# Layout of the stationary operand, the plan's lags and the end of a graph-network kernel on one Trainium2 core

## The chip, the cores and the metric

The kernel runs on one NeuronCore of a Trainium2 chip. The metric is the device time of one execution in microseconds. A ratio in this text is the mean time of one kernel's fast runs over the mean time of the other kernel's fast runs of the same rounds, with a 95% interval; it is therefore not quite the ratio of the medians that are quoted beside it. All runs here are of the fast state; small differences remain in the mean granted TensorE clock (0.989 to 0.998), and one section below is about them.

## The reference

Four layers on `x` of shape (64, 256, 128), all float32. The first three are graph convolutions with one 256 x 256 adjacency `adj`; each ends in `layernorm(x + layer(x))`. The fourth is a gated graph network of five steps, and most of the work is there:

```python
def step(h, _):
    m_in = jnp.einsum('nm,bmd->bnd', in_matrix, h)      # in_matrix = out_matrix = adj
    m_out = jnp.einsum('nm,bmd->bnd', out_matrix, h)
    av = jnp.concatenate([m_in, m_out], axis=-1)
    u3 = h @ u3_w.T + u3_b
    z = jax.nn.sigmoid(av @ w3_w.T + w3_b + u3)
    r = jax.nn.sigmoid(av @ w4_w.T + w4_b + u3)
    hv = jnp.tanh(av @ w5_w.T + w5_b + (r * h @ u5_w.T + u5_b))
    h = (1.0 - z) * h + z * hv
    return (h, None)
# ...
x = _layernorm(x + _L3_gnn_ref(x, adj, adj, ..., 5), axis=-1)
```

## The kernel before

The 64 batch entries form 32 groups of two. The kernel first writes down every operation of every group with a cost, a lag and its dependences (class `Plan`). A greedy simulation on the host, at build time, then orders them, and the instructions are emitted in that order. So **the plan's costs and lags are not executed; they only set the order on each engine**. On the chip an engine waits where the next operand of its list is late: in the trace of this kernel SyncE waited 138.6 us, in 85 waits, with a load of `h` for the write `dh` to land, and in the six traces compared below all its planned DMAs come in the planned order.

```python
ACTIVE = 6      # groups in flight
HEAD = 2        # the first groups turn x by TensorE
TAIL = 4        # the last groups turn h by TensorE (the "PE path")
...
    def add(self, engine, cost, lag, rank, run, reads=(), writes=(), after=()):
        op = Op(len(self.ops), rank, engine, cost, lag, run, [*reads, *writes])
...
def dve_cost(elements):
    return elements / 0.96 + 75          # 608 ns for 512 elements
```

The 608 ns are a number of the plan; in the trace VectorE's operations on 512 elements a partition took 683 to 723 ns by mean, and the transpose `th` of `hT`, which writes with a stride, 1111.

A step needs h in both orientations: `hT` (features on partitions) for the gates, and `h` (nodes on partitions) as the stationary operand of the propagation. `hT` is what the step produces. In most groups the way back to `h` is: VectorE transposes block by block (`th`, 1111 ns by mean), a DMA writes the blocks to DRAM (`dh`, 2.0 us from issue to landing by median), and a DMA reads them back in another order (`h`, 2.8 us). In the last `TAIL` groups TensorE transposes `hT` into PSUM instead (`pth`, four matmuls 109 ns apart) and ScalarE copies it out (586 ns by mean).

```python
        def turned(self, name, src, ins, outs):
            t, far = self.val("w", "t" + name), self.val("dram", "d" + name)
            self.dve(dve_cost(512), lambda: nc.vector.transpose(t.ap.rearrange(outs, k=4, q=Q),
                                                                src.ap.rearrange(ins, k=4, q=Q)), [src], [t])
            self.add("SP", 420, 2000, lambda: nc.sync.dma_start(far.ap, t.ap), [t], [far])
            return far

        def packed(self, name, src):
            far = self.turned(name, src, "p (k q i) -> p q k i", "p (k j q) -> p q k j")
            t = self.val("w", name)

            def run():
                nc.sync.dma_start(t.ap.rearrange("p (r n) -> p r n", r=4),
                                  far.ap.rearrange("(r i) (k n) -> (i k) r n", r=4, k=4))

            self.add("SP", 420, 2350, run, [far], [t])
            return t
...
    def by_node(v):                       # every 4th element of a row: 16 bytes apart
        return v.ap.rearrange("p (n q) -> p q n", q=Q)
...
            for s in range(STEPS):
                m = self.propagate(f"g{s}", h, ats, ins, outs)      # pmg, stationary operand h
                # ... pr, ph: ten matmul records of 512 columns; r, rh, z, hv; d, e ...
                hT = self.tensor(f"hT{s}", OP.add, hT, e)
                if g < G - TAIL:
                    if s < STEPS - 1:
                        h, ats, ins = self.packed(f"h{s}", hT), a1p, by_node
                else:
                    pT = self.transposes(f"h{s}", hT)
                    if s < STEPS - 1:
                        h = self.copied(f"h{s}", pT)
```

The four values of q in a row of `h` are interleaved there, so that the reading DMA can move runs of 512 bytes. The price is the stride in `by_node`: a weight load of this `h` takes 326 ns by mean, one of `y`, which lies in natural order, 190. (`a1p` is the adjacency with its rows in the order in which this DMA delivers the nodes; the views call it `aTp`.)

Of the kernel before, what the change touches and what calls it, by code (L numbers as in the profile page):

```python
# [14 lines left out]
NB = 2  # L15
ACTIVE = 6
HEAD = 2
TAIL = 4
STEPS = 5
EPS = 1e-5  # L20
BANKS = 8
# [20 lines left out]
class Plan:  # L42
# [7 lines left out]
        self.ops, self.slots = [], slots  # L50

    def add(self, engine, cost, lag, rank, run, reads=(), writes=(), after=()):
        op = Op(len(self.ops), rank, engine, cost, lag, run, [*reads, *writes])
        op.deps.update(after)
        for v in reads:
            op.deps.add(v.writer)
            v.readers.append(op)
        for v in writes:
            if v.writer is not None:
                op.deps.add(v.writer)  # L60
            op.deps.update(v.readers)
            v.writer, v.readers = op, []
        op.deps.discard(op)
        for v in op.vals:
            if op not in v.users:
                v.users.append(op)
        self.ops.append(op)
        return op
# [69 lines left out]
def act_cost(elements):  # L138
    return elements / 1.2 + 165
# [3 lines left out]
def kernel(  # L143
# [30 lines left out]
    nc = tc.nc  # L174
# [3 lines left out]
    Q = NB * T  # L178
# [125 lines left out]
    def nat(v):  # L304
        return v.ap.rearrange("p (q c) -> p q c", q=Q)
# [17 lines left out]
    class Group:  # L323
# [12 lines left out]
            return op  # L336

        def pe(self, cost, run, reads, writes):
            return self.add("PE", cost, 200, run, reads, writes)

        def dve(self, cost, run, reads, writes):
            return self.add("DVE", cost, 130, run, reads, writes)

        def act(self, run, reads, writes, cost=act_cost(512)):
            return self.add("ACT", cost, 70, run, reads, writes)

        def copied(self, name, ps, kind="w"):
            t = self.val(kind, name)
# [82 lines left out]
        def packed(self, name, src):  # L431


            far = self.turned(name, src, "p (k q i) -> p q k i", "p (k j q) -> p q k j")
            t = self.val("w", name)

            def run():
                nc.sync.dma_start(t.ap.rearrange("p (r n) -> p r n", r=4),
                                  far.ap.rearrange("(r i) (k n) -> (i k) r n", r=4, k=4))

            self.add("SP", 420, 2350, run, [far], [t])
            return t

        def product(self, ps, w, rhs, start, stop, shared=False):
# [13 lines left out]
        def record(self):  # L458
# [14 lines left out]
            for t in range(T):  # L473
                p = self.val("bank", f"py0{t}")
# [48 lines left out]
            h = y  # L523
            outs = None
            if g < G - TAIL:
                hT = self.brought("hT", self.turned("h", h, "p (q k j) -> p q k j", "p (k q i) -> p q k i"))
                outs = by_block
            else:
                pT = self.transposes("h", h)
                hT = self.val("w", "hT")  # L530
                self.dve(dve_cost(512), lambda t=hT, p=pT: nc.vector.tensor_copy(t.ap, p.ap), [pT], [hT])
            ats, ins = a1, None
            for s in range(STEPS):
                m = self.propagate(f"g{s}", h, ats, ins, outs)
                pr = self.val("bank", f"pr{s}")
                self.product(pr, u3T, hT, True, False)
                self.product(pr, w4T, m, False, True)
                r = self.gate_(f"r{s}", pr, AF.Sigmoid, rb)
                rh = self.tensor(f"rh{s}", OP.mult, r, hT)
                ph = self.val("bank", f"ph{s}")  # L540
                self.product(ph, w5T, m, True, False)
                self.product(pr, w34T, m, False, True, shared=True)
                z = self.gate_(f"z{s}", pr, AF.Sigmoid, zb)
                self.product(ph, u5T, rh, False, True)
                hv = self.gate_(f"hv{s}", ph, AF.Tanh, hb)

                d = self.tensor(f"d{s}", OP.subtract, hv, hT)
                e = self.tensor(f"e{s}", OP.mult, z, d)
                hT = self.tensor(f"hT{s}", OP.add, hT, e)
                if g < G - TAIL:  # L550
                    if s < STEPS - 1:
                        h, ats, ins = self.packed(f"h{s}", hT), a1p, by_node
                else:
                    pT = self.transposes(f"h{s}", hT)
                    if s < STEPS - 1:
                        h = self.copied(f"h{s}", pT)
            if g < G - TAIL:
                pT = self.brought("hn", self.turned("n", hT, "p (k q i) -> p q k i", "p (k q j) -> p q k j"))
                add = self.residual("3", pT, y, lambda v: v.ap.rearrange("p (r q j) -> p q r j", r=4, q=Q),
                                    lambda v: v.ap.rearrange("p (q r j) -> p q r j", r=4, q=Q))  # L560
            else:
                add = self.residual("3", pT, y)
            o = self.normalise("3", *add)
            self.add("SP", 450, 2700, lambda: nc.sync.dma_start(view(out, g), nat(o)), [o], [])

    a1 = [aT[:, kt, :] for kt in range(T)]
    a2 = [a2T[:, kt, :] for kt in range(T)]
    a1p = [aTp[:, kt, :] for kt in range(T)]
# [53 lines left out]
```

## Time and profile before

| | before |
|---|---|
| time, median of its first runs | 1457.4 us (1457.2 to 1458.1) |
| profiled span | 1455.1 us |
| TensorE busy | 97% |
| VectorE / ScalarE / GpSimd busy | 69% / 35% / 16% |
| DMA queue of SyncE, share of 16 engines | 26.2% |

The page's first part gives busy time, share of the span and number of instructions of each engine; its second part cuts the span into 40 slices and gives the busy tenths of each. In the views PE is TensorE, PEld its weight loads, DVE VectorE, ACT ScalarE, POOL GpSimd and SP SyncE. A line of the groups view reads: source line, engine, operation, out<-in by the program's names, shapes, count; then busy time in us and the mean duration of one in ns; then the idle time of the engine just before these instructions and what ended it. All matmuls come from one helper line, so the tile names tell them apart: `pmg` is the propagation in the gated network, `pr` and `ph` its gates, `pth` a transpose.

One measure in this text is not a line of a view: **PE's stalls**. Matmul durations overlap (those of `pmg<-aTp,h` are 402 ns by mean and start 233 ns apart), so I take the times from each matmul's start to the next one's, and take the median for each kind (mostly 216, 233, 429 or 109 ns); this median is called the pitch. The sum of the medians is the length that PE's stream would have without a wait; everything above it is stall. For the kernel before the sum is 5.4 us to the first matmul, 1391.2 us of medians, 50.1 us of stalls, and 8.4 us after the start of the last matmul: 1455.1 us.

### The profile page before, as it was taken

The numbers are of one execution on the slowest core, as the hardware profiler recorded it, in microseconds if no ns is written. First come the engines' busy times: TensorE is split into PE (matmuls) and PEld (weight loads), VectorE is DVE, ScalarE is ACT, GpSimd is POOL, SyncE is SP. The second block draws the span as 40 slices with busy tenths as digits, with TensorE's granted clock in tenths as the row PEclk, the third lists the DMA queues.
The fourth block names the chain that finished last, engine by engine and source line by source line (L and its number), as shares of the span: only waits on it lengthen the run. The fifth ranks groups of instructions, "written<-read, shape, count | busy, mean of one in ns | idle before, by whom it ended". The sixth has DMA issues, their size and how long they took to land.

```text
span 1455.1 us, 16313 instructions
## 1 busy us (share of the span) xinstructions
PE 1407.4 (97%) x5054; PEld 965.1 (66%) x5054; DVE 1008.5 (69%) x2696; ACT 515.7 (35%) x820; POOL 230.7 (16%) x199
## 2 busy tenths in 40 slices
PE   5999999999999999999999999999999999999995
PEld 4866676567666777667676667676677676656652
DVE  3756686758777686676876677776767768757734
ACT  1143423333333333333333333334333333344342
POOL 0411031101210122001211022111111112001200
PEclk9999999999999999999999999999999999999998
DMA  5022232323233223233222333223333322210000
GB/s 165 15 81 79 92 111 87 113 68 109 77 111 109 94 96 107 73 123 95 95 82 90 104 105 96 82 94 95 111 103 96 97 79 88 74 42 30 1 8 15
DMA packets 173830, 123.44 MB, mean 85 GB/s; under 512 B 12592, under 2 KB 148144, under 8 KB 173744
## 3 DMA queue, kind: packets, MB, share of 16 engines
q1 hardware_dynamic: 171440, 121.16, 26.2%
q10 hardware_dynamic: 2304, 1.25, 0.3%
q8 instruction: 40, 0.66, 0.2%
q14 instruction: 46, 0.38, 0.1%
HBM read 61.80 MB, written 60.29 MB: 84 GB/s over the span
## 4 chain that ended last, share of the span: by engine, by line
PE 47%; DVE 5%; DMA 1%; ACT 1%; issue 0%; POOL 0%; SPq 0%; POOLq 0%; DVEq 0%; ACTq 0%
PE pr L191 15%; PE pmg L191 10%; PE ph L191 10%; PE py L191 7%; PE pm L191 3%; PE pmq L191 1%; DVE y L382 1%; DMA h<-dh 1%; DVE d L455 1%; DVE e L455 1%; PE pth L406 1%; DVE st L357 1%; DVE hT L455 1%; ACT hv L449 0%; DVE s L373 0%
## 5 line engine op out<-in xcount | busy, mean ns | idle before, releaser
L368 POOL TENSOR_TENSOR rs<-ve,half 128x4 f32<-128x4 f32 x128 | 141.3, 1106 | 1120.3 <-DVE ve L362 1112.5
L191 PEld LDWEIGHTS pmg<-aTp,h 128*128 128x128 f32 x896 | 220.5, 326 | 39.0 <-DMA h<-dh 12.6
L191 PE MATMUL pmg<-aTp,h 128*128 128x256 f32 x896 | 231.1, 402 | 6.0 <-DMA h<-dh 5.6
L455 DVE TENSOR_TENSOR d<-hv,hT 128x512 f32<-128x512 f32 x160 | 114.3, 715 | 170.6 <-ACT hv L449 170.4
L455 DVE TENSOR_TENSOR rh<-r,hT 128x512 f32<-128x512 f32 x160 | 112.3, 702 | 143.2 <-ACT r L449 143.0
L349 ACT COPY mg<-pmg 128x512 f32<-128x512 f32 x160 | 93.7, 585 | 280.0 <-PE pmg L191 264.8
L382 DVE TENSOR_SCALAR y<-s,mv,rs 128x128 f32<-128x128 f32 x512 | 146.0, 350 | 56.5 <-POOL rs L368 56.0
L191 PE MATMUL pr<-hT,u3T 128*128 128x512 f32 x320 | 163.5, 596 | 3.5 <-DVE hT L455 3.1
L191 PE MATMUL pr<-mg,w4T 128*128 128x512 f32 x320 | 164.4, 595 | 2.3 <-ACT mg L349 2.3
L191 PE MATMUL pr<-mg,w34T 128*128 128x512 f32 x320 | 163.0, 594 | 0.1
L191 PE MATMUL ph<-mg,w5T 128*128 128x512 f32 x320 | 162.8, 592 | 0.0
L191 PE MATMUL ph<-rh,u5T 128*128 128x512 f32 x320 | 162.5, 593 | 0.0
L449 ACT ACTIVATE r<-pr,rb 128x512 f32<-128x512 f32 x160 | 110.0, 687 | 137.5 <-PE pr L191 129.0
L449 ACT ACTIVATE z<-pr,zb 128x512 f32<-128x512 f32 x160 | 109.9, 687 | 133.3 <-PE pr L191 128.4
L449 ACT ACTIVATE hv<-ph,hb 128x512 f32<-128x512 f32 x160 | 109.9, 687 | 48.3 <-PE ph L191 46.4
L414 DVE STREAM_TRANSPOSE th<-hT 128x512 f32<-128x512 f32 x112 | 124.4, 1111 | 1.4
L455 DVE TENSOR_TENSOR e<-z,d 128x512 f32<-128x512 f32 x160 | 115.6, 723 | 3.8
L455 DVE TENSOR_TENSOR hT<-hT,e 128x512 f32<-128x512 f32 x160 | 109.6, 686 | 2.5
L357 DVE BATCH_NORM_STATS2 st<-s 128x6 f32<-128x128 f32 x512 | 109.4, 278 | 1.2
L191 PEld LDWEIGHTS ph<-rh,u5T 128*128 128x128 f32 x320 | 60.4, 190 | 72.6 <-issue 56.9
L191 PEld LDWEIGHTS ph<-mg,w5T 128*128 128x128 f32 x320 | 60.8, 190 | 70.3 <-issue 56.7
L191 PEld LDWEIGHTS pr<-mg,w4T 128*128 128x128 f32 x320 | 59.0, 191 | 51.2 <-issue 43.8
(95 smaller groups left out, 1609.5 us busy)
## 6 DMA issues: line engine op xcount, KB each, us to landing
dh<-th SPq DMA_DIRECT2D x140, 256.0 KB, 2.0
h<-dh SPq DMA_DIRECT2D x112, 256.0 KB, 2.8
x<-in_x_dram SPq DMA_DIRECT2D x32, 256.0 KB, 3.4
out_dram<-y SPq DMA_DIRECT2D x32, 256.0 KB, 2.3
dx<-tx SPq DMA_DIRECT2D x30, 256.0 KB, 2.1
xT<-dx SPq DMA_DIRECT2D x120, 64.0 KB, 2.0
hT<-dh SPq DMA_DIRECT2D x112, 64.0 KB, 2.0
dn<-tn SPq DMA_DIRECT2D x28, 256.0 KB, 2.0
```

The costliest lines, as they stand in the source:

```text
L191: nc.tensor.matmul(o, lhsT, rhs, start=start, stop=stop, skip_group_check=shared)
L349: self.act(lambda: nc.scalar.copy(t.ap, ps.ap), [ps], [t])
L357: nc.vector.bn_stats(st.ap[:, q * 6:(q + 1) * 6], nat(s)[:, q, :])
L368: lambda: nc.gpsimd.tensor_tensor(rs.ap, ve.ap, half, op=OP.pow), [ve], [rs])
L382: nc.vector.tensor_scalar(nat(y)[:, q, :], nat(s)[:, q, :], mv.ap[:, 2 * q:2 * q + 1], rs.ap[:, q:q + 1], op0=OP.subtract, op1=OP.mult)
L406: nc.tensor.transpose(ps.ap[:, q * P:(q + 1) * P], src.ap[:, q * P:(q + 1) * P], ident)
L414: self.dve(dve_cost(512), lambda: nc.vector.transpose(t.ap.rearrange(outs, k=4, q=Q), src.ap.rearrange(ins, k=4, q=Q)), [src], [t])
L449: self.act(lambda: nc.scalar.activation(t.ap, ps.ap, func, bias=bias, scale=1.0), [ps], [t], act_cost(512) + 100)
L455: self.dve(dve_cost(512), lambda: nc.vector.tensor_tensor(t.ap, a.ap, b.ap, op=op), [a, b], [t])
```

## The change

The intent is to have `h` lie in natural order, so that the weight load reads a contiguous row; to tell the plan that results and transfers arrive later than it believed; and to use the PE path for the last two groups only.

```diff
-TAIL = 4
+TAIL = 2
...
     def add(self, engine, cost, lag, rank, run, reads=(), writes=(), after=()):
+        if engine == "SP":
+            lag += 700
...
-            return self.add("PE", cost, 200, run, reads, writes)
+            return self.add("PE", cost, 260, run, reads, writes)
...
-            return self.add("DVE", cost, 130, run, reads, writes)
+            return self.add("DVE", cost, 260, run, reads, writes)
...
-            return self.add("ACT", cost, 70, run, reads, writes)
+            return self.add("ACT", cost, 130, run, reads, writes)
...
-            far = self.turned(name, src, "p (k q i) -> p q k i", "p (k j q) -> p q k j")
+            far = self.turned(name, src, "p (k q i) -> p q k i", "p (k q j) -> p q k j")
...
-                nc.sync.dma_start(t.ap.rearrange("p (r n) -> p r n", r=4),
-                                  far.ap.rearrange("(r i) (k n) -> (i k) r n", r=4, k=4))
-
-            self.add("SP", 420, 2350, run, [far], [t])
+                f = far.ap.rearrange("(r i) (k q j) -> q (i k) r j", r=4, k=4, q=Q)
+                for q in range(Q):
+                    nc.sync.dma_start(nat(t)[:, q, :].rearrange("p (r j) -> p r j", r=4), f[q])
+
+            self.add("SP", 2570, 2000, run, [far], [t])
...
-                        h, ats, ins = self.packed(f"h{s}", hT), a1p, by_node
+                        h, ats, ins = self.packed(f"h{s}", hT), a1p, nat
```

The last SP line matters later: with the new load the plan also gets new figures for it, 1.8 us more than for the old one.

## The prediction

> **What bounds the kernel now.** I read the page's busy shares first, then the busy slices.
>
> ```profile
> span 1455.1 us, 16313 instructions
> PE 1407.4 (97%) x5054; PEld 965.1 (66%) x5054; DVE 1008.5 (69%) x2696; ACT 515.7 (35%) x820; POOL 230.7 (16%) x199
> PE   5999999999999999999999999999999999999995
> ...
> q1 hardware_dynamic: 171440, 121.16, 26.2%
> ```
>
> TensorE is busy in every slice but the first and last; VectorE has 31% to spare and the DMA queue of SyncE fills 26% of the DMA engines. So only three things can shorten the run: cheaper PE work, fewer PE stalls between 50 and 1350 us, and a shorter start or end. But ends of matmuls are modelled, so "busy" hides a slow stream. I therefore went to the groups by shape.
>
> ```profile
> L191 PE MATMUL pmg<-aTp,h 128*128 128x256 f32 x896 | 231.1, 402 | 6.0 <-DMA h<-dh 5.6
> L191 PEld LDWEIGHTS pmg<-aTp,h 128*128 128x128 f32 x896 | 220.5, 326 | 39.0 <-DMA h<-dh 12.6 <-PE pr L191 5.0 <-issue 4.7
> ...
> L414 DVE STREAM_TRANSPOSE th<-hT 128x512 f32<-128x512 f32 x112 | 124.4, 1111 | 1.4
> ...
> L191 PE MATMUL pmg<-aT,y 128*128 128x256 f32 x256 | 60.5, 379 | 0.0
> ...
> L191 PEld LDWEIGHTS pmg<-aT,y 128*128 128x128 f32 x256 | 48.5, 190 | 16.6 <-issue 6.9 <-PE pr L191 2.6 <-PE py L191 0.7
> ...
> L414 DVE STREAM_TRANSPOSE tn<-hT 128x512 f32<-128x512 f32 x28 | 19.8, 706 | 0.8
> ```
>
> The same product has two prices. With h packed (every fourth element) a weight load takes 326 ns, with natural y 190. [...] The timeline of PE gives what that costs, start to start (durations overlap, so starts are the measure):
>
> ```profile
> 702.29 2.03 PE L191 MATMUL pmg<-aTp,h 128*128 128x256 f32 x8
> 704.15 0.63 PE L191 MATMUL py<-w0s,xT 128*128 128x256 f32 x2
> ...
> 710.24 1.89 PE L191 MATMUL pm<-aT,y 128*128 128x256 f32 x8
> 711.97 0.39 PE L191 MATMUL pmg<-aTp,h 128*128 128x256 f32 x1
> ```
>
> Eight packed ones take 704.15 - 702.29 = 1.86 us (233 ns each, also the median of all 896 starts), eight natural ones 1.73 (216). Summing over the whole trace each start-to-start time above its kind's median gives PE's stalls: 11.1 us before 50 us, **23.8 us** from 50 to 1350, 15.2 us from 1350 to the last matmul, which is at 1446.7; 8.4 us of normalising and storing follow. Of the 23.8 us, 14.2 stand before or within pmg<-aTp,h and 6.3 before pr<-hT,u3T: late DMAs of h, and late VectorE results. The end, on PE's timeline:
>
> ```profile
> 1424.61 0.63 PE L406 MATMUL pth<-ident,hT 128*128 128x128 f32 x4 [1.46 <-DVE hT L455]
> ...
> 1435.42 0.66 PE L406 MATMUL pth<-ident,hT 128*128 128x128 f32 x4 [2.96 <-DVE hT L455]
> ...
> 1446.36 0.63 PE L406 MATMUL pth<-ident,hT 128*128 128x128 f32 x4 [3.05 <-DVE hT L455]
> ```
>
> The last two steps have one group alone: 10.8 and 10.9 us each, of which 6.5 (6.9 with the other group's last transposes) are PE work. A lone step loses about 4.3 us.
>
> [...] The trace has packets of 512 B (28 ns on average), 1 KiB (47) and 2 KiB (87), so 19.5 ns per 512 B over a fixed 8 or 9; of 128 B runs it shows nothing.
>
> **The change part by part.**
> 1. *Natural h.* Groups on the DMA path multiply by contiguous weights. Their step 0 (pmg<-aT,y, 216 ns) already pairs natural weights with the same blocked PSUM output, so nothing else in the form is new. 896 x (233 - 216) ns = **-15.2 us**, all on the bound engine. xT keeps its stride (231 ns), so py does not gain.
> 2. *Transposes.* Groups 28 and 29 leave the PE path: 24 transposes each (4 for y, 4 for each of 5 steps). The changed kernel's PE list is 12 rows of 4 shorter: 48 x 109 ns start to start = **-5.2 us**. Their ACT and VectorE copies go too, off the bound.
> 3. *VectorE.* th is now written unstrided: 112 x (1111 - 706) ns = 45 us less VectorE work, beside PE, and 0.4 us less latency per step.
> 4. *Load of h.* One DMA (issue 0.37 us, landing 2.8, at most 4.5) becomes four, each of 512 runs of 128 B. Four issues took 1.74 us for hn. 128 B at the rate fitted above costs some 13 ns a packet, and 28 if it is no cheaper than 512 B: 2048 packets over 16 engines are 1.7 to 3.6 us, against 0.9. So h should come 3.5 to 4.5 us after the first issue, some 1 to 1.5 us later than now after the gain of point 3. DMA busy share rises from 26% to an estimated 33 to 45%; SyncE issues about 165 us more in a run where it had 286. Neither is a bound.
> 5. *The plan's margins.* These change order alone. From hT to h the old plan allowed 738 + 2420 + 2770 = 5.9 us; the trace shows 1.1 + 2.0 + 2.8 plus issue waits, 6.0 at best: no margin, so half a microsecond more of queueing stalls PE. The new plan allows 868 + 3120 + 5270 = 9.3 us where I expect 6.5 to 7.5. It also had 608 ns for VectorE operations that last 690 to 720; a lag of 260 covers that. With six groups in flight, PE needs about 257 us for what one group must get through, so the longer way has other work to hide behind. I choose 24 us of stalls falling to about 10: **-14 us**, the softest term.
> 6. *The end.* In the changed order of PE, group 29 still has its last step when 35 us of PE work remain, and group 31 is alone for three steps, not two: +4.3 us, less about 1 for a calmer stretch before it. **+3 us**.
>
> Sum: 1457.4 - 15.2 - 5.2 - 14 + 3 = **1426.0 us**.
>
> **The rivals.**
> - *The stall term stays.* Same margin used up by slower loads, SyncE's in-order queue blocked by four issues at a time. For it: SyncE waits in order, and dh landings already reach 4.0 us where 2.0 is usual. Against: 2 us of spare in the plan. Then only the two sure terms and the end remain: about 1440.
> - *The 128-byte load becomes the bound.* If a packet cost 60 ns, one load would need 7.7 us and all 120 of them about 920 us of every DMA engine; loads would collide and PE starve: 1460 or more. Against: 28 ns for four times the bytes. I give it 5%.
> - *The end eats more.* Two more groups on the longer path when there is little other work: if groups 28 and 29 pull the last two later, six or more lone-step losses, +10 us, about 1433.
> - *Stalls vanish and the end is neutral:* -20 and 0 in place of -14 and +3: 1417.
>
> **Range and chances.** 2% faster means below 1428.2. The sure part, 20.4 us, is 1.4% and does not reach that alone; 8.8 us must come from stalls net of the end. I think that somewhat likelier than not. 8 in 10: 1416 to 1441. Faster 0.6, same 0.39, slower 0.01.
>
> **What would show it.** Right: weight loads of pmg<-aTp,h near 190 ns and its pitch 216; pth count 48 instead of 80, and 8 instead of 16 for y; th<-hT near 706 ns; stalls between 50 and 1350 us about 10 us, with waits for DMA h nearly gone; three lone steps of about 10.9 us at the end; h landing in 2 to 3.5 us from each issue; DMA share below 45%. Wrong: if pmg's pitch stays above 220, term 1 is wrong; if waits for DMA h grow, term 5 is, and the second rival if the DMA share is above 60%; if PE's last matmul comes more than 20 us of stalls after 1350 us' worth of work, term 6.

## The result

The changed kernel takes 1424.55 us (median; 1420.58 to 1426.45, 4 runs) against 1457.74 us (1457.19 to 1459.53, 4 runs). The ratio is 0.9767, interval 0.9742 to 0.9792: faster. The predicted 1426.0 us was 1.5 us off.

Busy shares and busy slices of the changed kernel's page, and its DMA queue of SyncE (packets, MB, share of the 16 engines):

```profile
span 1424.3 us, 16832 instructions
PE 1382.1 (97%) x5006; PEld 921.7 (65%) x5006; DVE 975.4 (68%) x2706; ACT 512.2 (36%) x812; POOL 230.5 (16%) x199
PE   5999999999999999999999999999999999999995
...
q1 hardware_dynamic: 369776, 127.47, 34.8%
```

PE is the bound as before and its share has not moved, because the span shrank with its work. The DMA queue carries more than twice the packets (369776 against 171440), and its share rose by less than nine points.

Groups by shape of the changed kernel:

```profile
L193 PE MATMUL pmg<-aTp,h 128*128 128x256 f32 x960 | 227.8, 381 | 0.0
L193 PEld LDWEIGHTS pmg<-aTp,h 128*128 128x128 f32 x960 | 183.2, 191 | 57.4 <-issue 26.3 <-PE pr L193 6.5 <-PE py L193 1.4
...
L416 DVE STREAM_TRANSPOSE th<-hT 128x512 f32<-128x512 f32 x120 | 84.2, 703 | 1.3
...
L408 PE MATMUL pth<-ident,hT 128*128 128x128 f32 x40 | 7.0, 303 | 12.0 <-DVE hT L458 12.0
```

Three things are to be seen. A weight load of h takes 191 ns. The waits for DMA h, which stood behind both lines before, are gone from them. The transposes of h are 40, half of the 80 before: my prediction had said 48, a slip, since four groups become two (its 48 was the number that goes away, 40 of hT and 8 of y).

PE's timeline in the middle of the changed kernel:

```profile
702.15 1.89 PE L193 MATMUL pmg<-aTp,h 128*128 128x256 f32 x8
703.88 1.02 PE L193 MATMUL pr<-hT,u3T 128*128 128x512 f32 x2
```

From 702.15 to 703.88 are 1.73 us for eight, 216 ns each, as for y.

PE's timeline at the end of the changed kernel, the starts of the steps of the last group:

```profile
1380.44 0.66 PE L408 MATMUL pth<-ident,hT 128*128 128x128 f32 x4 [0.69 <-DVE hT L458]
...
1391.42 1.11 PE L408 MATMUL pth<-ident,hT 128*128 128x128 f32 x4 [2.96 <-DVE hT L458]
1392.33 1.91 PE L193 MATMUL pr<-hT,u3T 128*128 128x512 f32 x2
1394.04 3.48 PE L193 MATMUL pmg<-aT,h 128*128 128x256 f32 x8
...
1405.13 0.63 PE L408 MATMUL pth<-ident,hT 128*128 128x128 f32 x4 [3.05 <-DVE hT L458]
...
1416.08 0.63 PE L408 MATMUL pth<-ident,hT 128*128 128x128 f32 x4 [3.05 <-DVE hT L458]
```

There are three lone steps, as the order had told: 11.0, 13.7 and 10.9 us. The middle one is new. Its matmuls take nearly twice as long (1.91 us for a pair of `pr`, 1.02 elsewhere). The windows view over the three steps shows why: its columns are the length, busy time and count of each engine, then the granted TensorE clock, the DMA share and GB/s.

```profile
1380.44:1391.42 10.98, 7.87 (x26) 3.81 (x26) 8.82 (x25) 3.27 (x6) 1.40 (x2) 0.95 0.17 49
1391.42:1405.13 13.71, 9.98 (x23) 5.30 (x23) 2.77 (x4) 3.23 (x5) 0.00 (x0) 0.79 0.00 1
1405.13:1416.08 10.95, 7.23 (x22) 3.48 (x23) 2.77 (x4) 3.23 (x5) 0.00 (x0) 1.00 0.00 0
```

The granted clock is 0.79 over the middle step: it was half from 1390.4 to 1397.2 us, for 6.8 us. The half clock began about 2 us into a pause of 2.96 us (1388.5 to 1390.4 us); through another pause, of 3.05 us at 1402 us, the clock stayed at 1.00. So the length of a pause alone does not tell in these traces whether the clock falls. The other stretches of half clock before the last matmul, at 25.1 and 1352.9 us here and at 24.1 us in the kernel before, are each 3.4 us long.

### The profile page after: what moved, and what is told of

The parts are those of the page before. It is cut to its first block, busy times and chain, and to the rows that moved or that the text cites. A ratio compares the mean times of both kernels' runs of the same rounds, so it can differ in the third digit from the quotient of the medians.

```text
span 1424.3 us, 16832 instructions
## 1 busy us (share of the span) xinstructions
PE 1382.1 (97%) x5006; PEld 921.7 (65%) x5006; DVE 975.4 (68%) x2706; ACT 512.2 (36%) x812; POOL 230.5 (16%) x199
## 3 DMA queue, kind: packets, MB, share of 16 engines
q1 hardware_dynamic: 369776, 127.47, 34.8%
## 4 chain that ended last, share of the span: by engine, by line
PE 93%; DVE 4%; DMA 1%; ACT 1%; POOL 0%; issue 0%; SPq 0%; POOLq 0%; DVEq 0%; ACTq 0%
PE pr L193 28%; PE pmg L193 19%; PE ph L193 19%; PE py L193 15%; PE pm L193 8%; PE pmq L193 3%; DVE y L384 1%; DVE st L359 1%; DMA x<-in_x_dram 1%; DVE d L458 0%; PE pth L408 0%; DVE hT L458 0%; DVE s L375 0%; DVE e L458 0%; DMA raw_w4T<-in_L_gnn_w_w_dram 0%; POOL rs L370 0%
## 5 line engine op out<-in xcount | busy, mean ns | idle before, releaser
L193 PE MATMUL pmg<-aTp,h 128*128 128x256 f32 x960 | 227.8, 381 | 0.0
L193 PEld LDWEIGHTS pmg<-aTp,h 128*128 128x128 f32 x960 | 183.2, 191 | 57.4 <-issue 26.3
L384 DVE TENSOR_SCALAR y<-s,mv,rs 128x128 f32<-128x128 f32 x512 | 150.2, 357 | 46.1 <-POOL rs L370 45.3
L193 PEld LDWEIGHTS pr<-mg,w34T 128*128 128x128 f32 x320 | 59.5, 190 | 53.6 <-issue 46.8
L193 PEld LDWEIGHTS pr<-hT,u3T 128*128 128x128 f32 x320 | 60.0, 191 | 43.3 <-issue 26.0
```

The lines of the kernel that those rows point to most:

```text
L193: nc.tensor.matmul(o, lhsT, rhs, start=start, stop=stop, skip_group_check=shared)
L384: nc.vector.tensor_scalar(nat(y)[:, q, :], nat(s)[:, q, :], mv.ap[:, 2 * q:2 * q + 1], rs.ap[:, q:q + 1], op0=OP.subtract, op1=OP.mult)
```

## The experiments

Each kernel was run with the same inputs and was correct. "Stalls, middle" are PE's stalls from 50 us to 100 us before the last matmul, "stalls, end" those of the last 100 us; both, and the sum of medians, come from the profiled run, whose time can differ by some us from the median.

| kernel | median us | ratio to before | sum of medians | stalls, middle | stalls, end |
|---|---|---|---|---|---|
| before | 1457.7 | 1 | 1391.2 | 23.8 | 15.2 |
| changed | 1424.6 | 0.9767 | 1371.2 | 7.5 | 21.5 |
| changed, again (x8) | 1423.6 | 0.9751 | 1370.3 | 7.5 | 18.6 |
| natural h only (x1) | 1428.0 | 0.9785 | 1375.9 | 10.8 | 15.1 |
| margins only (x2) | 1442.3 | 0.9883 | 1391.0 | 5.7 | 18.6 |
| PE path for two only (x3) | 1460.5 | 1.0011 | 1387.1 | 24.5 | 21.3 |
| natural h and margins (x4) | 1426.3 | 0.9772 | 1376.3 | 7.8 | 15.2 |
| plan knows the transpose (x5) | 1451.0 | 0.9934 | 1391.0 | 12.8 | 19.3 |
| natural h, old plan figures (x6) | 1445.5 | 0.9905 | 1376.3 | 23.7 | 16.8 |
| lone pauses filled (x7) | 1424.0 | 0.9752 | 1376.1 (filling in it) | 7.5 | 11.8 |
| PE path for one (x9) | 1428.4 | 0.9793 | 1367.8 | 9.2 | 15.9 |
| PE path for three (x10) | 1432.3 | 0.9823 | 1373.2 | 7.4 | 24.5 |
| last group first (x11) | 1430.4 | 0.9804 | 1370.7 | 11.0 | 18.2 |

The kernel before was run beside each of the three batches (x1 to x4; x5 to x8; x9 to x11): 1458.6, 1460.6 and 1457.5 us. The first batch ran on one chip and the other two on another, so kernels of different batches are best compared by their ratios.

### One part at a time (x1, x2, x3)

x1 is the kernel before with the changed `packed` (its plan figures 2570 and 2000 included) and `nat`, and nothing else:

```diff
 TAIL = 4                      # as before; lags 200 / 130 / 70, none added on SP
-            self.add("SP", 420, 2350, run, [far], [t])       # one DMA, by_node
+            self.add("SP", 2570, 2000, run, [far], [t])      # four DMAs, nat
```

> The kernel before with the natural h alone (four DMAs of 128-byte runs, contiguous weights, and the plan's own figures for that load, 2570 + 2000); old margins, four groups on the PE path. Theory: the pitch of pmg<-aTp,h falls from 233 to 216 ns, worth 15 us, and the stalls between 50 and 1350 us (23.8 us before, 9.7 after) stay at 17 us or more because the margins are what removes them: 1436 to 1443 us. Rival: the stalls come from the strided VectorE transpose, which the plan takes for 608 ns and which lasts 1111; natural h cures it, so stalls fall under 13 us without any margin: 1428 to 1433 us.

Measured: 1428.0 us (1427.4 to 1429.3). This falls in the rival's range, and the stalls of 10.8 us do too. The sum of medians fell by 15.3 us, as the pitch said it would; but 13.0 us of stalls went as well, without any margin. So the margins are not what it takes. Where PE and its weight loads sat idle before the instructions on `h`, both counted, in x1 (us, times):

```profile
its engine sat idle before it (us, times) until:
  issue: 28.0, 116
  PE pth L406: 11.2, 9
```

In the kernel before, the same view began with

```profile
  DMA h<-dh: 18.2, 30
```

In x1 it is not among the causes that the view lists.

x2 keeps packed h and takes the margins:

```diff
+        if engine == "SP":
+            lag += 700
-... PE 200, DVE 130, ACT 70
+... PE 260, DVE 260, ACT 130
```

> The kernel before with the plan's margins alone; packed h, pitch 233 ns, four groups on the PE path. Theory: stalls between 50 and 1350 us fall to about 10 us: 1442 to 1447 us. Rival (stalls come from the strided transpose): they stay above 18 us: 1452 us or more.

Measured: 1442.3 us (1441.5 to 1443.9), stalls 5.7 us, sum of medians unchanged. So margins alone remove the stalls too, 18.1 us of them. The two parts cure the same thing: 30.6 us for natural h and 16.3 for the margins (medians of their batch) would be 46.9 together, but x4, which has both, gained 32.3.

x3 changes one number:

```diff
-TAIL = 4
+TAIL = 2
```

> The kernel before with the PE path for the last two groups only, in place of four. Theory: 48 transposes less are -5.2 us, one more lone step at the end +4.3 us, up to 3 us more if the granted clock drops in the lone steps: 1455 to 1461 us, no change worth the name. Rival: the end costs 10 us, 1463 us or more; or it costs nothing, 1452.

Measured: 1460.5 us (1456.3 to 1465.4, 12 runs); ratio 1.0011, interval 0.9998 to 1.0024. The sum of medians is 4.1 us less and the stalls of the end 6.1 us more: the two cancel, as the theory said. The scatter of 9 us goes with the granted clock: 1456.3 us at 0.996 and 1465.4 at 0.991.

### Both without the end (x4)

```diff
-TAIL = 2                      # the changed kernel
+TAIL = 4
```

> The changed kernel with four groups on the PE path again (natural h and margins alone). Theory: +5.2 us of transposes, -4 us at the end, and no drop of the granted clock in the lone steps: 1422 to 1428 us, within noise of the changed kernel (1424.6). Rival: the two last groups' path is a real gain, 1429 or more.

Measured: 1426.3 us, all runs within 0.4 us, each at a clock of 0.995. The time is as forecast, but not the clock: the profile has half clock here too, from 1403.4 to 1406.8 us, after a pause of 3.44 us. So such a drop does not belong to the shorter PE path; of the kernels with four groups on it, x1, x2, x5 and x6 show one near the end as well, the kernel before none. Ratio 0.9772, against 0.9767 and 0.9751 for the changed kernel: the path of the last groups is worth between nothing and 3 us, inside the scatter.

### What does natural h cure the stalls with? (x5, x6)

x1 leaves two explanations: the VectorE transpose became as short as the plan believes (703 ns, plan 608, 1111 before), or the plan was told more of the load (1.8 us more in the plan, 1.2 us more on the chip: the last of the four DMAs lands 4.0 us after the first issue by median, one DMA before took 2.8). x6 has x1's work and the old figures:

```diff
-            self.add("SP", 2570, 2000, run, [far], [t])
+            self.add("SP", 420, 2350, run, [far], [t])
```

> Natural h alone (four groups on the PE path, no margins), but with the old plan figures for the load, 420 + 2350 in place of 2570 + 2000; the chip does the same work, only the order differs. Natural h alone with its own figures gave 1428.0 us and 10.8 us of stalls. Theory: what cured the stalls there was the plan's knowledge of the load (1800 ns more in the plan, about 1200 more on the chip), so here the load comes late: stalls of 20 us or more, 1436 to 1445 us. Rival: the shorter transpose (703 for 1111 ns) cured them; stalls stay at 13 us or less, 1427 to 1431 us.

Measured: 1445.5 us (1441.2 to 1450.1), half a microsecond above the theory's range, and stalls of 23.7 us in the profiled run, inside it: the theory holds, and the rival falls. The rows for `pmg` in x6's groups:

```profile
L191 PE MATMUL pmg<-aTp,h 128*128 128x256 f32 x896 | 216.8, 383 | 4.1 <-DMA h<-dh 3.5
L191 PEld LDWEIGHTS pmg<-aTp,h 128*128 128x128 f32 x896 | 166.5, 190 | 63.7 <-issue 19.1 <-DMA h<-dh 15.6 <-PE pr L191 4.5
```

The weight load is 190 ns and the pitch 216, and still PE and its weight loads, counted as above, wait for DMA h:

```profile
  DMA h<-dh: 19.1, 45
```

Two numbers of the plan, which no engine ever executes, are worth 17.5 us (1445.5 - 1428.0, two batches on two chips; by the ratios 0.9905 and 0.9785 it is the same). The scatter tells the same: 9 us at one and the same clock of 0.995, where x1 has 2 us.

x5 asks whether one wrong number on the old path is enough. The strided transpose of the kernel before is planned at what it takes:

```diff
-            far = self.turned(name, src, "p (k q i) -> p q k i", "p (k j q) -> p q k j")
+            far = self.turned(name, src, "p (k q i) -> p q k i", "p (k j q) -> p q k j", 1111)
-        def turned(self, name, src, ins, outs):
+        def turned(self, name, src, ins, outs, cost=dve_cost(512)):
-            self.dve(dve_cost(512), lambda: nc.vector.transpose(...
+            self.dve(cost, lambda: nc.vector.transpose(...
```

> The kernel before with one number of the plan changed: the strided VectorE transpose of h is planned at its measured 1111 ns in place of 608; nothing else, packed h, old margins. Theory: half a microsecond that the plan does not know of, on a path without margin, makes the stalls: they fall from 23.8 to 15 us or less, 1445 to 1451 us. Rival: the stalls come from scatter of landings and of queueing, so half a microsecond in the plan is not enough: 20 us or more, 1454 us or more.

Measured: 1451.0 us, stalls 12.8 us. Half a microsecond in the plan takes away 11 us of stalls. In its waits (who waited for what: us in total, times, longest us) DMA h is down from 12.6 us to

```profile
PEld pmg L191 <- DMA h<-dh: 4.2, 9, 1.1
```

So the stalls in the middle are not set by the layout, the DMA or VectorE alone: figures of the plan bring them back (x6 against x1) and take them away (x2, x5). The traces also show the slack itself. Replaying the plan on the host gives SyncE's planned DMAs in the order that the traces have, every one of them in these six kernels, so each landing of `h` can be paired with its `hT` (medians, us):

| kernel | hT to h, in the plan | hT to h, on the chip | h lay ready before its first matmul | stalls, middle |
|---|---|---|---|---|
| before | 6.4 | 6.7 | 0.9 | 23.8 |
| x6 | 6.4 | 7.9 | -0.2 (started before the last quarter landed) | 23.7 |
| x5 | 6.9 | 6.7 | 1.2 | 12.8 |
| x1 | 8.3 | 7.6 | 1.7 | 10.8 |
| x2 | 7.8 | 6.7 | 2.4 | 5.7 |
| changed | 9.8 | 7.9 | 3.3 | 7.5 |

Where the plan's way is shorter than the chip's, there are 24 us of stalls; where it is longer, 13 us or less. Half a microsecond takes away about half of them (x5), and more slack most of them (x1, x2). What these runs do not separate: x1 and x5 raise a planned cost, which in the plan also keeps SyncE or VectorE occupied, and x2 raises lags alone, but on every engine. No run changed only a lag on this path.

### The end (x7, x9, x10, x11)

x7 fills two of the lone pauses of the changed kernel with matmuls whose result nobody reads, to see whether the clock then stays up:

```diff
                 self.product(ph, u5T, rh, False, True)
+                if g == G - 1 and s in (2, 3):
+                    spare = self.val("bank", f"spare{s}")
+                    for _ in range(3):
+                        self.product(spare, u5T, rh, True, True)
```

> The changed kernel with three matmuls into a spare bank, whose result nobody reads, after the last product of steps 2 and 3 of the last group, where PE waits 3 us for VectorE. Theory: the pauses of the lone steps let the granted clock fall to half for the step after (1390.4 to 1397.2 us in the changed kernel); filled, the clock holds, the lone steps take 10.9 us each, and the time is 2 to 4 us below the changed kernel on the same chip, with less scatter. Rival: the clock falls all the same, or the filling delays the step: same or slower.

> The changed kernel once more, on the same chip as the filled one. 1420 to 1427 us; runs with a mean granted clock of 0.996 near 1421, those of 0.993 near 1426.

Measured: 1424.0 us (1422.3 to 1425.2) and 1423.6 us (1421.4 to 1426.8). The windows over the three lone steps of the filled kernel:

```profile
1379.49:1390.48 10.99, 10.45 (x33) 4.96 (x33) 8.82 (x25) 3.27 (x6) 1.40 (x2) 1.00 0.16 49
1390.48:1401.32 10.84, 9.79 (x29) 4.62 (x29) 2.77 (x4) 3.23 (x5) 0.00 (x0) 1.00 0.00 2
1401.32:1412.30 10.98, 7.25 (x23) 3.50 (x23) 2.77 (x4) 3.23 (x5) 0.00 (x0) 1.00 0.00 0
```

The clock holds at 1.00, and the middle step takes 10.8 us, where it took 13.7 in one profile of the changed kernel and 12.5 in the other. So far it is as expected, but the forecast of the time was a miss: 2 to 4 us less did not appear. The profile of x8 shows one reason. It happened to run its start without the drop to half clock that the other changed kernel's profile and x7's had at about 25 us, and was 2.7 us ahead of x7 when the lone steps began. Two of these three profiles have the drop at the start and one has not, and with four runs each that hides a gain of this size. It stays open whether the filling is worth 2 us.

x9 and x10 change the number of groups on the PE path:

```diff
-TAIL = 2
+TAIL = 1                      # x9;  TAIL = 3 in x10
```

> The changed kernel with the PE path for the last group only. In its order group 30 and the last group end together (4 us of PE work apart), so hardly a step is lone in the sense of one group's work; but group 30 is now on the long path, and there is little else to run while its h is on its way. Theory (each group moved to the DMA path saves 2.6 us of transposes and costs the end about as much or more): 1422 to 1428 us, stalls in the last 100 us of 20 us or more. Rival: the end shortens because both last groups finish together, 1418 us or less.

> The changed kernel with the PE path for the last three groups. 2.6 us more of transposes, and the last lone stretch is 13.8 us of PE work in place of 20.2, so two lone steps and not three: -4.3 us at the end. Theory: 1420 to 1425 us, at most 2 us better than the changed kernel, stalls in the last 100 us about 15 us. Rival: no gain, 1425 or more.

x9: 1428.4 us, 0.4 us above the forecast, and not by its reason: stalls of the end are 15.9 us, fewer than with two groups. The time went behind PE: the last matmul starts at 1408.5 us of 1426.6, so 18.1 us follow where 8 did, since the result of group 30 now goes through DRAM before it can be normalised. x10: 1432.3 us, a miss by 7 us. It has two lone steps as its order told, but the groups before them leave one wait of 5.4 us for hT at 1343 us, with 6.8 us of half clock around it, and two more of 2.2 us. The count of lone steps is not enough to forecast an end.

x11 puts the last group ahead of groups 29 and 30 where the plan can choose:

```diff
-            op = plan.add(engine, cost, lag, self.g, run, reads, writes, after)
+            op = plan.add(engine, cost, lag, 28.5 if self.g == 31 else self.g, run, reads, writes, after)
```

> The changed kernel with the last group ahead of groups 29 and 30 where the plan has to choose between ready operations. Groups 29 and 30 then end last, 6 us of PE work apart. If the end costs what the lone steps of one group cost, it shortens, to 1416 to 1421 us; if the long path of group 29 takes their place as the wait, it is 1425 us or more, which I hold likelier, since a step on that path waits about 10 us for its h.

Measured: 1430.4 us (1427.7 to 1432.0), in the range that I held likelier, but not for its reason: after 1290 us PE waits 11.9 us in four waits for hT of VectorE and never for a DMA of h. (The expectation's 10 us of waiting for h was an estimate; in the changed kernel the way from hT to h took 7.9 us by median, and 3.3 us more passed until the first matmul of h.) Why this order is slower stays open. No version tried is better than the changed kernel beyond its scatter.

## Why the prediction was right, point by point

In the profiles the span fell by 30.8 us: 20.0 us of medians and 16.3 us of stalls in the middle went, 6.3 us of stalls came at the end, and the rest is under 1 us. The prediction had 20.4, 14 and 3. Its two soft terms missed by 2.3 and 3.3 us in opposite directions; that the total came within 1.5 us is in part luck.

1. *Natural h, -15.2 us: right.* The pitch is 216 ns in every kernel that has it, and the sum of medians fell by 15.3 us in x1.
2. *Transposes, -5.2 us: right.* The sum of medians fell by 5.1 us from x4 to the changed kernel, and by 4.1 in x3, where 64 matmuls of the two groups became packed as well (64 x 17 ns = 1.1 us).
3. *VectorE: right, somewhat too large.* th<-hT takes 703 ns where it took 1111, and its busy time fell from 124.4 to 84.2 us though there are 120 of it and no longer 112; VectorE in all is 33 us less busy. Its shorter latency alone did not help (x6).
4. *The load of h: right, with SyncE under-estimated.* A 128-byte packet took 12.9 ns on average (I had 13 by the fit; one of 512 bytes took 28.3), a load of 64 KB in 128-byte runs landed 2.4 us after its issue by median (2.0 us in 512-byte runs), the last landing came 4.0 us after the first issue (3.5 to 4.5), and the share is 34.8% (33 to 45). SyncE's issues took 501 us where I had 286 + 165. The whole way from hT to h took 7.9 us by median where I had 6.5 to 7.5; the new plan's 9.3 us and more covered it.
5. *"The plan's margins ... -14 us": right in size, wrong in whose it is.* Stalls in the middle fell from 23.8 to 7.5 us, or to 9.7 counted to 1350 us as in the prediction. I gave all of it to the margins. The runs show that natural h alone brings 13 us of it along, by way of the plan's figures for its load, and that the margins add about 3 us on top (x1 10.8 us of stalls, x4 7.8). I had read the two numbers 2570 + 2000 as a description of the load and not as slack; with 5.9 us planned for a way of "6.0 at best" I had the right diagnosis in hand and did not see that any lengthening would do. (The trace has 5.8 us at best and 6.7 by median, so the plan was further off than I said.) The total came out right because the prediction counted the common gain once.
6. *The end, +3 us: somewhat short, and a cause was missing.* The three lone steps are there. The stalls of the last 100 us rose by 6.3 us in one profile and 3.4 in the other (counted from 1350 us as in the prediction, to 19.2 us in the first, just under the 20 that it named as a sign of being wrong); of the 6.3, about 2.8 us are the middle step's half clock, which the prediction did not have. The net of steps 2 and 6, forecast at -2.2 us, is between +1.9 (x3) and -2.7 us (x4 to the x8 run): nothing that can be told from zero here.

The rivals: stalls did not stay, since the load did not use up the plan's slack; the DMA did not become a bound at 12.9 ns a packet; the end did eat more, by 3.3 us in one profile and 0.4 in the other, where that rival allowed 7.

## What to carry to other kernels

Compare start-to-start times of the same matmul with different operand layouts before trusting busy shares; here the strided stationary operand showed as a weight load of 329 ns by median against 190, and its matmuls of 256 columns started 233 ns apart in place of 216. Where a static plan orders the engines, check its figures against the trace along each whole path, because half a microsecond of missing slack cost about 10 us here (x5), and take out one part at a time before crediting it, since two parts may supply the same slack. At the end of a kernel, count what follows the last matmul and the pauses of the lone steps together; moving one of them moved the other.
